# FFN transform over 512 blocks of 4 tokens, Toeplitz products in four row groups of the array

## The chip, the core and the metric

The kernel runs on one core of one Trainium2 chip. The metric is device time in microseconds (us) for one launch, the median of several runs. The launch contains two layers; the change touches only the second part of the second layer and the steps that prepare it.

## What is computed

The first layer is a windowed attention block on a (2, 128, 64, 64) image. The second layer is a self-attention over the same 4096 tokens of each of two images, followed by a spectral FFN. The change concerns the FFN. Cut to what matters:

```
# u: (2, 4096, 128); phi: (4096, 16); K = 16 filters
U_plus [b,t,k,d]  = sum_s phi[t-s, k] * u[b,s,d]             # causal convolution in time
U_minus[b,t,k,d]  = (-1)^t * sum_s phi[t-s, k] * (-1)^s u[b,s,d]
out[b,t,e] = sum_k sum_d U_plus*sigma_k^0.25*Mpp[k,d,e] + U_minus*sigma_k^0.25*Mpm[k,d,e]
out += three short lags of u times Mu[lag];   one of 4 branch weights per segment of tokens
```

Even and odd times are kept apart (the parity `par`, 2048 tokens each), so that plus and minus share one set of products.

## The kernel before

**How the convolution is tiled.** Each parity's 2048 tokens are CB = 256 blocks of FB = 8 tokens. Along the blocks a Fourier transform of length NC = 320 is taken (a matmul with a table `tr`), which leaves BINS = 160 complex bins. For each bin the convolution inside a block is a small Toeplitz product; then the 16 filters are contracted with the mixed matrices `mpl` and `mmi`, and the bins go back to tokens with a matmul against `inv`.

**Where the pieces run.**

- `after(b, c, part)` (16 calls, spread through the attention of layer 2 as filler work, one yielded piece at a time) normalises 512 tokens, transposes them, does the forward transform and stores the bins to the DRAM tensor `us`. Each call makes two 512-wide products per half table (L1034), copies them out by DVE and ACT (L1036) and stores them, with a smaller remainder (L1044, L1050).
- `filters()` transforms the filter taps (L1195), sums them (L1202, L1205) and stores them to the DRAM tensor `gs`.
- `short_lags` adds the three short lags into the residual `xa` (L1082, L1089).
- `group()` loads nothing itself: `blocks(q)` and `inputs(q)` have loaded `ct` (Toeplitz blocks) and `ut` (transformed tokens) four pairs of bins ahead. For each of 2 pairs of bins, 2 parities and 2 images it makes two 64-row Toeplitz products of 512 columns, one in each half of the array's rows (L1381), each into its own PSUM tile `pc`. DVE copies one, ACT the other, into `y` (L1382). The `ps_c` pool has 6 PSUM tiles.
- `project` contracts one of the 16 filters for a group of GB = 4 bins: 256 columns at full array (L1393), 16 with `mpl` and 16 with `mmi` into one PSUM tile `acc`; the last one is followed by one ACT copy into `ob` (L1400).
- `back_into` (32 calls in two steps each, slipped between projections from group 16 on) takes 64 bins back into the residual: 2 transposes (L1409), an ACT copy, 2 products of 256 columns (L1415), one DVE addition (L1417).
- The tail turns the last 32 bins (L1456), adds them and the residual (L1466, L1470, L1474, L1475) and stores the output in four DMAs of 1 MB.

**Other lines that are referred to.** L509 is the score product of the first layer's windowed attention (32 rows, four heads), L604 a 128-column product there; L383 and L398 are small DVE operations of a layer norm there. In the second layer, L905 is the attention's score product, L929 turns a tile of its exponentials by TensorE, L932 copies that out and sums it by DVE, and L943 and L970 are the products with the tokens. In `after`, L1002 is a DVE operation of 128 elements and L1015 the ACT copy of the transposed tokens into `zc`, with 32 bytes between words.

**What sets the order.** TensorE's order in the FFN is written out by hand (`manual_schedule`): first the Toeplitz products of group g+1, then the 32 projections of group g, and so on for 40 groups. DVE's and ACT's instructions stand in the order of the program text. All loads and stores of this part are issued on SP's queue.

Of the kernel before, what the change touches and what calls it, by code (L numbers as in the profile page):

```python
# [82 lines left out]
CB, FB, SG = 256, 8, 4  # L83
SB = CB // SG
NC = CB + SB

CHUNKS = (0, 1, 4, 5, 2, 3, 6, 7)
BINS = NC // 2
GB = 4
BC = 64  # L90
LG = 2 * FB
GROW = 4 * LG * KF


@with_exitstack
def kernel(
# [100 lines left out]
    def token_tiles(b, n0, pt):  # L197
        for j in range(4):
            ph, f = divmod(n0 + j, FB)
            par, h = divmod(ph, 2)  # L200
            t0 = h * TH + 2 * f + par
            nc.tensor.transpose(
                pt[:, j * P : (j + 1) * P], xa[b][:, t0 : t0 + 2 * FB * (P - 1) + 1 : 2 * FB], ident
            )
# [21 lines left out]
    with l0a:  # L226
# [449 lines left out]
        halves = [n0 for h in range(2) for n0 in range(0, NT, 4) if n0 // FB % 2 == h]  # L676
# [177 lines left out]
    t_in, t_filter, t_out = _transforms()  # L854


    us = dram.tile([BINS, 2, SG, FB, NB, 2, P], F32, name="us")
    gs = dram.tile([BINS, 2, SG, GROW], F32, name="gs")

    with ap_:  # L860
# [10 lines left out]

        tr = tp.tile([P, 2, NC], F32, name="tr")
        nc.sync.dma_start(out=tr, in_=nc.inline_tensor(t_in, "t_in").ap().rearrange("(h p) c -> p h c", p=P))
# [116 lines left out]
        def after(b, c, part):  # L990

            n0 = 4 * c
            ph, f0 = divmod(n0, FB)
            par, h = divmod(ph, 2)
# [6 lines left out]
            for j in range(4):  # L1001
# [12 lines left out]
            s0 = 1 + h * (TH // 2)  # L1014
            nc.scalar.copy(  # L1015
                zc[b][:, par, s0 : s0 + TH // 2].rearrange("p (c f) -> p f c", f=FB)[:, f0 : f0 + 4, :],
                pt.rearrange("p (f c) -> p f c", f=4),
            )
            yield
            z2 = z.rearrange("p f d -> p (f d)")  # L1020

            def store(m0, q, src):
                nc.sync.dma_start(
                    out=us[m0 // 2 : (m0 + P) // 2, :, 2 * h + q, f0 : f0 + 4, b, par, :].rearrange(
                        "g r f d -> (g r) f d"
                    ),
                    in_=src.rearrange("p (f d) -> p f d", d=P),
                )

            for m0 in (0, P):  # L1030
                for q in range(2):
                    rows_ = slice(q * SB, (q + 1) * SB)
                    pu = bank()
                    nc.tensor.matmul(pu, lhsT=tr[rows_, h, m0 : m0 + P], rhs=z2[rows_], start=True, stop=True)  # L1034
                    ub = sp.tile([P, 512], F32, tag="ub", name="ub", bufs=3)
                    (nc.scalar.copy if q else nc.vector.tensor_copy)(ub, pu)  # L1036
                    store(m0, q, ub)
                yield

            banks = [bank() for q in range(2)]  # L1040
            for i in range(2):
                for q in range(2):
                    rows_ = slice(q * SB, (q + 1) * SB)
                    nc.tensor.matmul(  # L1044
                        banks[q][i * 64 : (i + 1) * 64, 0:256], lhsT=tr[rows_, h, 2 * P : NC],
                        rhs=z2[rows_, i * 256 : (i + 1) * 256], start=True, stop=True,
                    )
            ub = sp.tile([P, 512], F32, tag="ub", name="ub", bufs=3)
            for q in range(2):
                (nc.scalar.copy if q else nc.vector.tensor_copy)(ub[:, q * 256 : (q + 1) * 256], banks[q][:, 0:256])  # L1050
                for i in range(2):
                    nc.sync.dma_start(
                        out=us[P:, :, 2 * h + q, f0 + 2 * i : f0 + 2 * i + 2, b, par, :].rearrange("g r f d -> (g r) f d"),
                        in_=ub[i * 64 : (i + 1) * 64, q * 256 : (q + 1) * 256].rearrange("p (f d) -> p f d", d=P),
                    )
# [7 lines left out]
        def short_lags(b, h):  # L1063


            for par in range(2):
                n0 = (par * 2 + h) * FB
                for f0 in range(0, FB, 4):
                    pt = bank()
                    transposed(pt, tt[b][:, n0 + f0 : n0 + f0 + 4, :])  # L1070
                    nc.scalar.copy(xa[b][:, (n0 + f0) * P : (n0 + f0 + 4) * P], pt)
                    yield
            for par in range(2):
                n0 = (par * 2 + h) * FB
                xv = xa[b][:, n0 * P : (n0 + FB) * P].rearrange("p (f c) -> p f c", f=FB)
                for c0 in range(0, P, 64):
                    py = lag_bank()
                    for lag in range(3):
                        from_par = (par - lag) % 2
                        back = (lag - par + from_par) // 2  # L1080
                        s0 = 1 + (h * P + c0) * FB - back
# [3 lines left out]
                    pv = py.rearrange("p (c f) -> p f c", f=FB)  # L1085
                    first = h == 0 and c0 == 0
                    for lo, hi, s in ((0, 32, 0), (32, 64, 1)) if first else ((0, 64, 2 + h),):
                        xs = xv[:, :, c0 + lo : c0 + hi]
                        nc.vector.scalar_tensor_tensor(  # L1089
                            xs, pv[:, :, lo:hi], seg[:, s : s + 1], xs, ALU.mult, ALU.add  # L1090
                        )
# [75 lines left out]
        def filters():  # L1167
# [44 lines left out]
            for slot in range(begin[-1] + SG):  # L1212
                mine = [(m, slot - s0) for m, s0 in enumerate(begin) if 0 <= slot - s0 < SG]
                for mj in mine:
                    more(*mj)
# [359 lines left out]
```

## Time and profile before

| what | us |
|---|---|
| median of 3 runs | 2191.98 (2191.19 to 2192.96) |
| span of the profiled execution, first to last instruction | 2190.3 |
| TensorE busy | 2142.9 (98%) |
| DVE busy / ACT busy / GpSimd busy | 953.2 / 769.8 / 278.7 |
| before the FFN's first Toeplitz product | 0 to about 1284 |
| FFN, 40 groups | about 1284 to 2165 |
| tail | about 2165 to 2190 |

The profile holds one execution; the median of the runs is 1.7 us above its span. In the profile a 32-bit float matmul shows as two records, each preceded by a weight load (PEld), so that counts of matmuls there are twice those of the program text. A group's line gives the number of instructions, the busy time, the mean duration of one in ns, and the idle time of its engine just before them with what ended that idle time.

### The profile page before, as it was taken

Reading aid. Unit: us, or ns where it says so; the run is one execution under the profiler, and the core shown is the slowest. Engines: PE = TensorE matmul, PEld = TensorE weight load, DVE = VectorE, ACT = ScalarE, POOL = GpSimd, SP = SyncE. Lnnn points to the kernel's source line nnn. Section 1 sums busy time; section 2 is a strip of 40 time slices with the busy share of each in tenths; the row PEclk is TensorE's granted clock in tenths of the full one; section 3 lists DMA queues with packets and bytes.
Section 4 is the critical chain, followed back from the end, with each engine's and each line's share of the span. In section 5 each row is a group of like instructions: output and inputs, shape, how many; then the busy total and the mean of one; then the engine's idle time right before and its main releaser. Section 6 shows DMA issues by size and latency. Waiting matters only on the chain.

```text
span 2190.3 us, 32068 instructions
## 1 busy us (share of the span) xinstructions
PE 2142.9 (98%) x12016; PEld 1341.7 (61%) x12016; DVE 953.2 (44%) x3150; ACT 769.8 (35%) x1904; POOL 278.7 (13%) x359
## 2 busy tenths in 40 slices
PE   6899999999999999999999999999999999999998
PEld 4677765545555544544555456776767676767776
DVE  5899986444443353366333543222232323232232
ACT  3889883222332232122223223223232323232232
POOL 3477874200000000000000000000000000000000
PEclk8999999999999999999999999999999999999999
DMA  4222212011000010042000132121221212222101
GB/s 147 61 62 62 61 53 53 0 68 53 25 24 25 24 49 25 0 139 87 0 24 26 47 112 56 44 60 45 55 56 44 53 47 48 53 46 54 40 10 77
DMA packets 170347, 110.56 MB, mean 50 GB/s; under 512 B 21311, under 2 KB 155087, under 8 KB 169680
## 3 DMA queue, kind: packets, MB, share of 16 engines
q1 hardware_dynamic: 169266, 105.01, 17.7%
q8 instruction: 95, 1.56, 0.3%
q0 software_dynamic: 576, 2.10, 0.3%
q10 hardware_dynamic: 350, 1.41, 0.2%
q14 instruction: 60, 0.49, 0.1%
HBM read 73.86 MB, written 34.63 MB: 50 GB/s over the span
## 4 chain that ended last, share of the span: by engine, by line
PE 87%; DVE 5%; POOL 3%; DMA 2%; ACT 1%; issue 1%; SPq 0%; ACTq 0%; POOLq 0%; DVEq 0%
PE acc L1393 26%; PE pc L1381 13%; PE own L943 10%; PE bank L905 9%; PE other L970 8%; PE bank L929 4%; PE bank L335 2%; PE bank L1082 2%; PE bank L545 2%; PE bank L195 2%; PE bank L1034 1%; PE py L1415 1%; DMA st<-in_m_minus_dram 1%; PE bank L509 1%; PE po L567 1%; ACT p L532 1%
## 5 line engine op out<-in xcount | busy, mean ns | idle before, releaser
L1382 DVE COPY y<-pc 128x512 f32<-128x512 f32 x320 | 221.5, 692 | 350.7 <-PE pc L1381 347.0
L913 ACT ACTIVATE e<-bank 128x512 f32<-128x512 f32 (+3 forms) x288 | 161.6, 561 | 510.0 <-PE bank L905 393.6
L1393 PE MATMUL acc<-y,mpl 128*128 128x256 f32 x1280 | 292.2, 383 | 0.0
L1393 PE MATMUL acc<-y,mmi 128*128 128x256 f32 x1280 | 288.1, 380 | 0.0
L1381 PE MATMUL pc<-ct,ut 64*128 64x512 f32 x1280 | 285.5, 596 | 0.0
L905 PE MATMUL bank<-cm 128*128 128x512 f32 (+3 forms) x576 | 277.5, 564 | 1.4 <-DVE y L656 1.4
L1393 PEld LDWEIGHTS acc<-y,mpl 128*128 128x128 f32 x1280 | 238.8, 190 | 58.7 <-issue 29.5
L1393 PEld LDWEIGHTS acc<-y,mmi 128*128 128x128 f32 x1280 | 243.3, 191 | 31.9
L1382 ACT COPY y<-pc 128x512 f32<-128x512 f32 x320 | 204.6, 640 | 92.3 <-PE pc L1381 92.2
L943 PE MATMUL own<-et,tok 128*128 128x512 f32 x448 | 227.8, 595 | 4.2 <-DVE part L932 4.2
L970 PE MATMUL other<-e,tok 128*128 128x512 f32 x448 | 229.1, 593 | 0.3 <-DVE xa L982 0.3
L1381 PEld LDWEIGHTS pc<-ct,ut 64*128 64x128 f32 x1280 | 120.7, 187 | 145.8 <-issue 140.6
L932 DVE CUSTOM_DVE_ANT_0 et<-bank,one 128x512 f32<-128x512 f32 x224 | 146.0, 687 | 120.3 <-PE bank L929 120.2
L1400 ACT COPY ob<-acc 128x256 f32<-128x256 f32 x32 | 19.0, 594 | 387.0 <-PE acc L1393 387.0
L943 PEld LDWEIGHTS own<-et,tok 128*128 128x128 f32 x448 | 84.0, 190 | 113.5 <-issue 66.6
L1417 DVE TENSOR_TENSOR xa<-py,xa 128x512 f32<-128x512 f32 x32 | 22.2, 693 | 281.4 <-PE py L1415 281.4
L970 PEld LDWEIGHTS other<-e,tok 128*128 128x128 f32 x448 | 82.0, 191 | 89.9 <-issue 87.1
L929 PEld LDWEIGHTS bank<-ident,e 128*128 128x128 f32 x896 | 102.8, 141 | 54.3 <-issue 49.0
L905 PEld LDWEIGHTS bank<-cm 128*128 128x128 f32 x576 | 94.1, 191 | 64.5 <-issue 44.1
L167 POOL TENSOR_TENSOR ln_rs<-ln_rs,mhalf 128x4 f32<-128x4 f32 x24 | 24.2, 1007 | 773.4 <-DVE ln_rs L166 773.4
L532 ACT ACTIVATE p<-p,mn 128x196 f32<-128x196 f32 x256 | 114.4, 449 | 13.6 <-DVE mn L522 13.1
L929 PE MATMUL bank<-ident,e 128*128 128x128 f32 x896 | 117.3, 274 | 0.0
(227 smaller groups left out, 2344.3 us busy)
## 6 DMA issues: line engine op xcount, KB each, us to landing
ut<-us SPq DMA_DIRECT2D x80, 256.0 KB
us<-ub SPq DMA_DIRECT2D x64, 256.0 KB
vw<-vd SPq DMA_DIRECT2D x256, 49.0 KB
ct<-gs SPq DMA_DIRECT2D x160, 72.0 KB
ct<-gs SPq DMA_DIRECT2D x160, 64.0 KB
gs<-sum SPq DMA_DIRECT2D x20, 256.0 KB
vd<-v SPq DMA_DIRECT2D x128, 32.0 KB
st<-in_m_plus_dram SPq DMA_DIRECT2D x16, 256.0 KB
```

Of the source, the lines that this page charges most:

```text
L195: nc.tensor.transpose(ps[:, j * P : (j + 1) * P], src[:, j, :], ident)
L335: nc.tensor.matmul(pl, lhsT=wg[:, lo : lo + P], rhs=zT, start=True, stop=True)
L532: nc.scalar.activation(p, p, AF.Exp, bias=t[name + "mn"][:, h : h + 1], scale=-1.0, accum_out=t["den"][:, u, h : h + 1],)
L905: nc.tensor.matmul(ps[:, lo:], lhsT=cm[b][:, n * P : (n + 1) * P], rhs=cm[b][:, CHUNKS[c] * 512 + lo : (CHUNKS[c] + 1) * 512], start=True, ...
L913: nc.scalar.activation(e[:, lo:], ps[:, lo:], AF.Exp, bias=0.0, scale=ASCALE, accum_out=part[:, n, c : c + 1])
L929: nc.tensor.transpose(pt[:, k * P : (k + 1) * P], es[k][:, m * P : (m + 1) * P], ident)
L932: nc.vector.tensor_tensor_reduce(et, pt, one, 1.0, 0.0, ALU.mult, ALU.add, part[:, n, a : a + 1])
L943: nc.tensor.matmul(own, lhsT=tok[b][:, n, :], rhs=e, start=first, stop=last)
L970: nc.tensor.matmul(other, lhsT=tok[b][:, 4 * CHUNKS[a] + j, :], rhs=es[j], start=(j == 0), stop=(j == 3))
L1381: nc.tensor.matmul(pc, lhsT=ut[fp, b, par, :], rhs=cv_[fp], start=True, stop=True)
L1382: (nc.scalar.copy if f else nc.vector.tensor_copy)(y[:, 4 * f : 4 * f + 4, :, par, b * 2 * FB + q : (b + 1) * 2 * FB : 2], pc.rearrange("p ...
L1393: nc.tensor.matmul(acc, lhsT=(mmi if l else mpl)[:, k, :], rhs=y[:, 1::2, k, ::-1, :] if l else y[:, 0::2, k, :, :], start=(l == 0 and k = ...
```

## The change

The sizes change: FB = 4 tokens to a block, CB = 512 blocks, NC = 640, K2 = 80 steps over quadruples of bins (a group is still two loads, 40 groups).

- **Forward transform, radix 2.** Even and odd blocks are transformed apart (`tr` has a table for each, e = 0, 1) and combined as sum and difference. In `after`, each bank of PSUM holds both halves; ACT copies one half to SBUF (`half`), DVE makes the sum and the difference (`ub`), and there are 16 stores per call on SP's queue where there were 8. In `filters`, the sums are made by ACT and DVE as before, the sum and difference and a negated copy by GpSimd, with 32 stores where there were 20.
- **Toeplitz products in four row groups.** `burst` makes, per load and parity, 2 images x 4 bins of 32-row products of 256 columns; the four bins j go to four row groups and four PSUM tiles `pcs[j]`. Each tile is full after both images and is then copied into `y` by DVE (j even) or ACT (j odd). Per group there are two bursts, one ahead of the 16 `mpl` projections and one ahead of the 16 `mmi` projections.
- **`y` changes its layout**: the bin is now the innermost index, with 8 of them, so a copy writes words 32 bytes apart (they were 8 bytes apart).
- **Backward transform, radix 4.** `mixed_bins` replaces the copy after a group's last projection: one ACT copy of 256 columns, then eight DVE operations (two of 128 elements, two of 64, four of 32) that write the four quarters into `ob`.
- `back_into` has 16 calls, with 4 transposes, one ACT copy of 512, 4 products of 128 columns and 2 DVE additions of 256. The tail turns 16 remaining quadruples and adds them in 32-row products of 64 columns.

```diff
-CB, FB, SG = 256, 8, 4
+FB, SG = 4, 4
+CB = TH // FB
...
-GB = 4
+KG = 8 // FB
+GB = 4 * KG
...
         def after(b, c, part):
...
-            for m0 in (0, P):
-                for q in range(2):
-                    rows_ = slice(q * SB, (q + 1) * SB)
-                    pu = bank()
-                    nc.tensor.matmul(pu, lhsT=tr[rows_, h, m0 : m0 + P], rhs=z2[rows_], start=True, stop=True)
-                    ub = sp.tile([P, 512], F32, tag="ub", name="ub", bufs=3)
-                    (nc.scalar.copy if q else nc.vector.tensor_copy)(ub, pu)
-                    store(m0, q, ub)
-                yield
+            def store(pu, n, r0, m, ri):
+                for s in range(2):
+                    half = sp.tile([P, 256], F32, tag="uo", name="uo", bufs=2)
+                    nc.scalar.copy(half[:, 0:n], pu[s][:, n : 2 * n])
+                    ub = sp.tile([P, 2, 256], F32, tag="ub", name="ub", bufs=4)
+                    for sgn, op in enumerate((ALU.add, ALU.subtract)):
+                        nc.vector.tensor_tensor(ub[:, sgn, 0:n], pu[s][:, 0:n], half[:, 0:n], op)
+                    for sgn in range(2):
+                        to = us[r0 : r0 + m, sgn, :, 2 * hh + s, 2 * fp : 2 * fp + 2, b, par, :]
...
-        def group(other=None):
-            y = cp.tile([P, 8, KF, 2, 32], F32, tag="y", name="y", bufs=2)
-            for q in range(GB // 2):
+        def burst(y, i):
+            for kl in range(i * (KG // 2), (i + 1) * (KG // 2)):
                 ct, ut = ahead.pop(0)
...
+                for pars in at_once:
+                    pcs = [ps_c.tile([P, 4, 2 * len(pars), TK], F32, tag="pc", name="pc") for _ in range(4)]
+                    for x, (par, b) in enumerate((par, b) for par in pars for b in range(NB)):
+                        cv_ = ct[:, :, 0 : 2 * (FB + 1 + par) * KF].rearrange("p o (l c) -> p o l c", l=2)[:, :, :, 0:TK]
+                        for j in range(4):
+                            rows_ = slice(32 * j, 32 * j + 32)
+                            nc.tensor.matmul(
+                                pcs[j][:, :, x, :], lhsT=ut[rows_, b, par, :], rhs=cv_[rows_], start=True, stop=True
                             )
+                    for j in range(4):
+                        if FB == 4:
+                            to = y[:, :, :, pars[0], :, 4 * kl + j]
...
+                        (nc.scalar.copy if j % 2 else nc.vector.tensor_copy)(
+                            to, pcs[j].rearrange("p l x (t k) -> p l k (x t)", k=KF)
+                        )
...
+        def new_y():
+            return cp.tile([P, 4, KF, 2, 2 * FB, GB], F32, tag="y", name="y", bufs=2)
...
+        def mixed_bins(g, acc):
+            af = cp.tile([P, 256], F32, tag="af", name="af", bufs=2)
+            nc.scalar.copy(af, acc)
+            av = af.rearrange("p (m s) -> p m s", s=2)
+            sd = cp.tile([P, 2, 128], F32, tag="sd", name="sd", bufs=2)
+            for s, op in enumerate((ALU.add, ALU.subtract)):
+                nc.vector.tensor_tensor(sd[:, s, :], av[:, :, 0], av[:, :, 1], op)
...
+            nc.vector.tensor_tensor(to[0], sv[:, 0], sv[:, 1], ALU.add)
+            nc.vector.tensor_tensor(to[1], sv[:, 0], sv[:, 1], ALU.subtract)
+            nc.vector.tensor_tensor(to[2][:, 0], dv[:, 0, 0], dv[:, 1, 1], ALU.subtract)
+            nc.vector.tensor_tensor(to[2][:, 1], dv[:, 0, 1], dv[:, 1, 0], ALU.add)
+            nc.vector.tensor_tensor(to[3][:, 0], dv[:, 0, 0], dv[:, 1, 1], ALU.add)
+            nc.vector.tensor_tensor(to[3][:, 1], dv[:, 0, 1], dv[:, 1, 0], ALU.subtract)
...
-            for g in range(BINS // GB):
-                following = group() if g + 1 < BINS // GB else None
-                acc = ps_p.tile([P, 64 * GB], F32, tag="acc", name="acc")
+            for g in range(GROUPS):
+                following = new_y() if g + 1 < GROUPS else None
+                acc = ps_p.tile([P, 256], F32, tag="acc", name="acc")
                 for l in range(2):
+                    if following is not None:
+                        burst(following, l)
                     for k in range(KF):
                         project(g, y, acc, l, k)
-                        if rest and k in ((3, 11) if g >= 2 * BC // GB else (7,)):
+                        if rest and k in (5, 13):
                             if next(rest[0], None) is None:
                                 rest.pop(0)
+                mixed_bins(g, acc)
                 y = following
```

The rest of the diff carries the new sizes through the token order (`token_tiles`, `short_lags`), the filter stores, the tables and the tail. In the compiled order of the changed kernel, DVE's eight operations of `mixed_bins(g)` stand ahead of the copies of the burst that follows group g's last projection.

## The prediction

> **What bounds the kernel now.** I read the page's busy line and chain first, then the chain of waits inside a stretch of the FFN, then the timeline at the start of one group.
>
> ```profile
> PE 2142.9 (98%) x12016; PEld 1341.7 (61%) x12016; DVE 953.2 (44%) x3150; ACT 769.8 (35%) x1904; POOL 278.7 (13%) x359
> ```
>
> ```profile
> 8 pieces in order of time: start us, us, what
> ...
> 1469.46 14.01 PE acc L1393 x64
> 1483.47 7.07 PE pc L1381 x32
> 1490.54 14.01 PE acc L1393 x64
> 1504.55 7.07 PE pc L1381 x32
> ```
>
> TensorE is never idle in the FFN: a group is 7.07 us of Toeplitz products and 14.01 us of projections, 21.08 us, 40 times. In the groups (line, engine, tile, shape; busy us, mean ns; idle before), DVE and ACT wait for TensorE, never the reverse:
>
> ```profile
> L1381 PE MATMUL pc<-ct,ut 64*128 64x512 f32 x1280 | 285.5, 596 | 0.0
> L1382 DVE COPY y<-pc 128x512 f32<-128x512 f32 x320 | 221.5, 692 | 350.7 <-PE pc L1381 347.0
> L1382 ACT COPY y<-pc 128x512 f32<-128x512 f32 x320 | 204.6, 640 | 92.3 <-PE pc L1381 92.2
> L509 PE MATMUL bank<-kT,qT 32*64 32x196 f32 x1024 | 43.3, 359 | 1.1 <-DVE mn L522 0.8 <-ACT pT L552 0.2
> ```
>
> The timeline shows what a group begins with; the copies start about 1.2 us after the products (1505.68 against 1504.48), here 0.03 to 0.07 us after the record of the product they need ends:
>
> ```profile
> 1504.48 3.28 PE L1381 MATMUL pc<-ct,ut 64*128 64x512 f32 x14
> 1504.59 0.59 ACT L1400 COPY ob<-acc 128x256 f32<-128x256 f32 x1 [13.34 <-PE acc L1393]
> ...
> 1505.68 0.64 ACT L1382 COPY y<-pc 128x512 f32<-128x512 f32 x1 [0.50 <-PE pc L1381]
> 1505.71 1.48 DVE L1382 COPY y<-pc 128x512 f32<-128x512 f32 x2 [14.45 <-PE pc L1381]
> ```
>
> **What the skill says.** "TensorEngine Tiling (Array Packing)", Performance Considerations: after a 4x speedup of TensorE the PSUM copy may become the bottleneck. In this trace two row groups already halve the time and the copies (692 and 640 ns) fit inside a pair's 2 x 442 ns; with four row groups they no longer do. "TensorE: Matmul & The Clock Gate", Part 3, gives 3.07x for four 32-row products. The trace has 32-row products too: L509 takes 43.3 us for 512 products of 196 columns, 85 ns each; at full array they would take 196 / 256 x 432 = 331 ns (64 records of L1393 come every 0.216 us), so the trace shows 3.9x. I use four. "Vector Engine (DVE) Microarchitecture Reference", 5.2, says a stream whose every element lands away from the last is slower: 1.71 ns per column for a destination hopping 4 KiB, 2.50 for steps of 24 words, against 1.05. The trace agrees in kind: L1015 writes words 32 bytes apart, L1475 16 bytes apart, and both cost about 400 ns more than 512 contiguous words (L1417, 693):
>
> ```profile
> L1417 DVE TENSOR_TENSOR xa<-py,xa 128x512 f32<-128x512 f32 x32 | 22.2, 693 | 281.4 <-PE py L1415 281.4
> L1475 DVE TENSOR_TENSOR o<-py,xa 128x512 f32<-128x512 f32 x8 | 8.8, 1102 | 12.9 <-PE py L1470 11.3 <-DMA out_dram<-o 1.6
> L1015 ACT COPY zc<-bank 128x512 f32<-128x512 f32 x8 | 8.7, 1082 | 17.2 <-PE bank L195 17.2
> ```
>
> **Part 1: Toeplitz products and their copies.** The new `y` is written 32 bytes apart. So an ACT copy costs 1.08 us (L1015, the same step) and a DVE copy 1.10 us (L1475). Bounds: 0.69 us if the step costs nothing; 512 x 2.50 + 160 = 1.44 us at the page's worst rate, 160 ns being what 693 leaves over 512 x 1.04.
>
> A burst has 2 parities of 8 products in 4 tiles. One image's four products are two waves of records, each 256 columns, 0.216 us (L1393), so a parity is four waves; the first wave of a switch shows 0.32. The last wave starts at 0.32 + 0.216 x 2 = 0.75 and its record lasts 0.38: tiles are full at 1.13 us. There are 6 PSUM tiles. The second parity takes the two free ones at once, but its third product waits for DVE's copy of the first tile, and behind it on TensorE stand the rest of the burst and 16 projections. Undisturbed, DVE starts at 1.16, ends at 2.26, TensorE resumes at 2.32 (0.06 for the signal, as between the ends and starts above) and needs 0.32 + 3 x 0.216 = 0.97: burst 3.29 us.
>
> For the burst after a group's last projection DVE is not free. `mixed_bins` stands ahead in its queue: ACT starts 0.11 after the switch (L1400), 0.37 for 256 contiguous columns (L1050), DVE begins at 0.52. Two operations of 128 elements at 0.26 (pitch of L1002's), two of 64 at about 0.19, four of 32 at about 0.13 (between L398's 0.17 and L383's pitch of 0.07) and 0.15 for two waits on its own results give 1.57: DVE is free at 2.1, its copy ends at 3.2, TensorE resumes at 3.26, burst 4.2 us.
>
> Both bursts: 7.5 us against 7.07, although the products alone would take 3.5. Projections are unchanged at 14.0. That is +0.43 x 39 groups = **+17 us**. With the copy at 0.69 us the bursts are 2.88 and 3.8, -0.4 x 39 = -16; at 1.44 us they are 3.63 and 4.55, +1.1 x 39 = +43. Loads (`ct`, `ut`): as many on SP's queue, `ct` half the bytes, issued four loads ahead; hidden behind the projections.
>
> **Part 2: back into the residual.** Before, 32 places of 2 transposes (0.109 each) and 4 records of 0.216: 1.08 x 32 = 35 us on TensorE, on the path. After, 16 places of 4 transposes and 8 records of 0.112 (the pitch of L604's 128-column records): 1.33 x 16 = 21. **-13 us**. The ACT copy and DVE additions lie beside projections.
>
> **Part 3: before the FFN.** Columns in `after` are the same on TensorE. DVE's work grows from 2 x 0.69 + 0.43 = 1.8 us to 8 x 0.36 + 4 x 0.22 = 3.8 a call, 16 calls, +32 us, and `short_lags` splits each addition in four, +0.4 x 16. In 700 to 1284 us DVE is below half busy and TensorE idles little, so attention's products cover it, except where a queued attention operation of DVE comes late. `filters` saves about 5 us of columns (20 x 512 to 24 x 256, two at a time) but makes DVE wait up to 1.8 us for GpSimd's sums six times; behind DVE stand attention's turned tiles (L932), for which L943 waits. I set these against each other with +3. The last `after` calls have no cover: SP issues 16 stores at 0.4 to 0.6 us (before, 8), so the first `ut` load, behind them on SP's queue, goes some 3 us later. Sum **+6 us**, bounds -4 and +22 (a fifth of DVE's added work exposed, and the end twice as long).
>
> **Part 4: tail.** The last `mixed_bins` takes 2.1 us where an ACT copy took 0.6 before the transposes (L1456): +1.5. Four output steps of 4 banks each, out of 6, wait for the previous step's copies (3 x 0.6 us of strided words): about +0.5 each, and the last copies end 1 us later. **+4 us**, bounds 0 and +8.
>
> **Sum.** +17 - 13 + 6 + 4 = +14 us on a span of 2190.3; with the 1.7 by which the median stands above it, **2206 us**. A measurement of this kernel can tell about 0.2%, 4.4 us, from no change.
>
> **Rivals.**
> - *The copies keep their speed* (0.69 us, ACT alike). For it: the step of 8 bytes in the old `y` costs DVE nothing. Against: L1015 and L1475. Then -16 - 13 + 6 + 4 = -19: 2173 us. This decides the sign: with everything else as above, the break-even is a DVE copy of about 0.92 us (each 0.1 us is 0.1 x 78 = 8 us). Chance, with a shorter `mixed_bins` or full cover in part 3, 0.2.
> - *Copies at the worst rate*, +43 instead of +17: 2232 us. For it the page's 2.50; against it that all strided rows here stand near 1.1. Chance 0.15, with DVE's added work exposed in the attention (+15).
> - *The four row groups do not run together*, only two at a time: each parity 0.86 us longer, partly under the copy's wait, +0.9 x 78 = +70: about 2275 us. L509's rows speak against it. 0.05.
> - *No visible change*, the gains of part 2 meeting the losses: 2187.6 to 2196.4, 0.1.
>
> **How the numbers follow.** The likeliest case, 2196 to 2225, has 0.5; slower in all 0.7, same 0.1, faster 0.2. Its own range is 2196 to 2225; 8 in 10 need the lower half of the worst-rate case and the nearer half of the faster one: 2177 to 2245.
>
> **What would show it.** Right: L1424 products with 4 starts within some 20 ns, TensorE idle before or within L1424 released by DVE's L1432, about 0.9 us in one burst and 1.8 in the other; L1432 near 1.1 us on both engines; L1483 half of L1415's time; a group of about 21.5 us. Wrong: L1432 near 0.7 us, or bursts near 3 us, or new idle time of L943 before 1284 us beyond some 10 us.

## The result, and the profile after

The changed kernel takes 2207.6 us (median of 4 runs, 2206.5 to 2211.0); the kernel before takes 2192.5 beside it. The ratio is 1.0070, 95% interval 1.0055 to 1.0084: 0.7% slower. The profiled execution has a span of 2206.3 us, 16.0 more than before's 2190.3. The prediction was 2206.

The page of the changed kernel, its busy line and its costliest groups (busy us, mean ns of one; idle us before them and what ended it):

```profile
PE 2068.9 (94%) x13704; PEld 1376.1 (62%) x13704; DVE 1111.1 (50%) x3680; ACT 872.6 (40%) x1942; POOL 306.9 (14%) x391
...
L1432 ACT COPY y<-pc 128x512 f32<-128x512 f32 x320 | 317.8, 1109 | 308.8 <-PE pc L1424 295.0
L1432 DVE COPY y<-pc 128x512 f32<-128x512 f32 x320 | 313.3, 1081 | 222.6 <-PE pc L1424 222.6
...
L1424 PE MATMUL pc<-ct,ut 32*128 32x256 f32 x2560 | 220.6, 404 | 78.1 <-DVE y L1432 74.9
```

TensorE was busy for 98% of the span and is now busy for 94%. Its Toeplitz products cost less, but it stands idle among them for 78.1 us, and 74.9 of these end when DVE has copied a full tile into `y`. The copies went from 692 and 640 ns to 1081 and 1109.

The chain of waits of the changed kernel over one group of the FFN (start us, us, what):

```profile
1480.88 0.38 ACT af L1452
...
1481.29 0.49 DVE sd L1456 x2
...
1482.46 0.99 DVE y L1432
...
1483.50 1.13 PE pc L1424 x12
1484.63 7.10 PE acc L1444 x32
1491.73 1.11 PE pc L1424 x16
1492.85 1.06 DVE y L1432
...
1493.95 1.17 PE pc L1424 x12
1495.12 1.06 PE acc L1444 x4
```

Before, this chain was TensorE alone. Now each of the two bursts passes through DVE: the second through one copy of 1.06 us, the first through ACT's copy of `acc`, `mixed_bins` and then the copy. Between them stand 7.10 us for 16 projections (32 records of the profile).

The difference of 16.0 us, placed by three moments that both traces show:

| moment | before, us | after, us | stretch up to it, after less before | predicted |
|---|---|---|---|---|
| first Toeplitz product | 1283.9 | 1295.6 | +11.7 | +6 |
| last projection | 2164.0 | 2179.6 | +3.9 (FFN 880.1, now 884.0) | +17 - 13 = +4 |
| end of the span | 2190.3 | 2206.3 | +0.4 | +4 |

The first row compares one execution with one. In e1_rows, e2_spread and e3_later, whose program is the changed kernel's up to there, the first Toeplitz product lies at 1294.3, 1296.4 and 1291.9 us, so the +11.7 can be anything from +8 to +12.5.

### The profile page after: what moved, and what is told of

Read it like the earlier page. It is cut to its first block, busy times and chain, and to the rows that moved or that the text cites. A ratio compares the mean times of both kernels' runs of the same rounds, so it can differ in the third digit from the quotient of the medians.

```text
span 2206.3 us, 36375 instructions
## 1 busy us (share of the span) xinstructions
PE 2068.9 (94%) x13704; PEld 1376.1 (62%) x13704; DVE 1111.1 (50%) x3680; ACT 872.6 (40%) x1942; POOL 306.9 (14%) x391
## 3 DMA queue, kind: packets, MB, share of 16 engines
q1 hardware_dynamic: 180738, 94.13, 15.2%
## 4 chain that ended last, share of the span: by engine, by line
PE 70%; DVE 12%; issue 9%; DMA 4%; POOL 3%; ACT 2%; SPq 1%; POOLq 0%; DVEq 0%; ACTq 0%
PE acc L1444 18%; PE own L958 10%; PE bank L920 9%; PE other L985 7%; PE pc L1424 6%; DVE y L1432 4%; PE bank L944 4%; PE bank L345 2%; PE bank L555 2%; PE bank L203 1%; PE bank L1060 1%; DMA st<-in_m_plus_dram 1%; DMA st<-in_m_minus_dram 1%; PE bank L519 1%; PE bank L1103 1%
## 5 line engine op out<-in xcount | busy, mean ns | idle before, releaser
L1432 ACT COPY y<-pc 128x512 f32<-128x512 f32 x320 | 317.8, 1109 | 308.8 <-PE pc L1424 295.0
L1432 DVE COPY y<-pc 128x512 f32<-128x512 f32 x320 | 313.3, 1081 | 222.6 <-PE pc L1424 222.6
L1424 PE MATMUL pc<-ct,ut 32*128 32x256 f32 x2560 | 220.6, 404 | 78.1 <-DVE y L1432 74.9
L1444 PEld LDWEIGHTS acc<-y,mmi 128*128 128x128 f32 x1280 | 238.7, 190 | 43.2 <-issue 12.9
L1424 PEld LDWEIGHTS pc<-ct,ut 32*128 32x128 f32 x2560 | 149.2, 185 | 145.0 <-DVE y L1432 108.0
L542 ACT ACTIVATE p<-p,mn 128x196 f32<-128x196 f32 x256 | 114.4, 449 | 12.9 <-DVE mn L532 12.3
L1456 DVE TENSOR_TENSOR sd<-af 128x128 f32<-128x128 f32 x80 | 19.7, 288 | 194.6 <-ACT af L1452 194.6
L1452 ACT COPY af<-acc 128x256 f32<-128x256 f32 x40 | 14.9, 372 | 212.9 <-issue 164.9
```

Of the source, the lines that this page charges most:

```text
L542: nc.scalar.activation(p, p, AF.Exp, bias=t[name + "mn"][:, h : h + 1], scale=-1.0, accum_out=t["den"][:, u, h : h + 1],)
L1424: nc.tensor.matmul(pcs[j][:, :, x, :], lhsT=ut[rows_, b, par, :], rhs=cv_[rows_], start=True, stop=True)
L1432: (nc.scalar.copy if j % 2 else nc.vector.tensor_copy)(to, pcs[j].rearrange("p l x (t k) -> p l k (x t)", k=KF))
L1444: nc.tensor.matmul(acc, lhsT=(mmi if l else mpl)[:, k, :], rhs=y[:, l::2, k, ::-1] if l else y[:, l::2, k], start=(l == 0 and k == 0), sto ...
```

## The experiments

My theory after the result had two halves. In the FFN, the copies' 32-byte steps and DVE's queue ahead of them hold TensorE. Ahead of the FFN, where the miss lies, I suspected first DVE's added work, then SP's added stores, then the buffers of the matrix loads. Line numbers of experiments can differ by one or two from those of the changed kernel.

### Is it the 32-byte step? (e1_rows)

```diff
-                            to = y[:, :, :, pars[0], :, 4 * kl + j]
+                            to = y[:, :, :, pars[0], 4 * kl + j, :]
...
-            return cp.tile([P, 4, KF, 2, 2 * FB, GB], F32, tag="y", name="y", bufs=2)
+            return cp.tile([P, 4, KF, 2, GB, 2 * FB], F32, tag="y", name="y", bufs=2)
```

ACT's copy of `acc` restores the order.

> Only the layout of y is changed: bin ahead of block position, so that a copy writes runs of 8 adjacent words; the ACT copy of acc puts the columns back in the old order. Theory (the 32-byte step doubles the copies, and the copies hold the PSUM tiles for which the second parity waits): L1432 falls to about 0.69 us on DVE and 0.64 on ACT, each burst shortens by about 0.4 us (3.39 and 3.83 to about 3.0 and 3.4), 78 bursts, -31 us: about 2176 us, faster than the kernel before the change (2192). Rival (the copies are slow because DVE and ACT write the same tile at once, or read PSUM with a 64-byte step): L1432 stays at 1.1 us, time within 5 us of 2207.

Measured: 2174.0 us, ratio to before 0.9912 (0.9896 to 0.9929). The page of e1_rows, the groups of the copies:

```profile
L1432 DVE COPY y<-pc 128x512 f32<-128x512 f32 x320 | 205.8, 684 | 262.7 <-PE pc L1424 262.6
L1432 ACT COPY y<-pc 128x512 f32<-128x512 f32 x320 | 171.9, 589 | 377.3 <-PE pc L1424 377.3
```

The copies are at their old speed with the same number of elements, the bursts fall from 3.83 and 3.39 us to 3.44 and 2.97, and TensorE's idle time in the products behind DVE's copies from 74.9 to 44.9. DVE and ACT still write one tile at once and still read PSUM with the same step, so the rival of the expectation falls. The step of 32 bytes costs some 400 ns a copy on DVE and 520 on ACT, and it decides the sign of the whole change: without it the kernel is 0.9% faster than before, with it 0.7% slower.

### Does TensorE need to wait for a copy at all? (e2_spread)

The two parities of a burst, which stood one behind the other, stand eight projections apart.

```diff
-                    if following is not None:
-                        burst(following, l)
                     for k in range(KF):
+                        if following is not None and k % 8 == 0:
+                            burst(following, l, (k // 8,))
                         project(g, y, acc, l, k)
```

> Only TensorE's order is changed: the two parities of a burst are put 8 projections apart, instead of one behind the other; copies and layout as they were. Theory (the gain of four row groups goes into a wait for PSUM tiles): TensorE's idle time in L1424 (78 us) is gone, four half bursts of 0.97 to 1.05 us and four runs of 8 projections of 3.55 us give a group of about 18.3 us instead of 21.4, -3.1 x 39 = -121 us: about 2086 us. Rival (the loss is in the switches between 32-row and 128-row products): twice as many switches at about 0.2 us each add 0.4 x 39 = 16 us: about 2223 us. Rival (DVE and ACT become the bound): 10.3 us of DVE copies and sums a group would have to grow to 18, which is not expected.

Measured: 2110.5 us, ratio to before 0.9620 (0.9606 to 0.9634). The chain of waits of e2_spread in the FFN:

```profile
1470.26 1.08 PE pc L1424 x16
1471.34 3.65 PE acc L1446 x16
1474.99 1.07 PE pc L1424 x16
1476.06 3.65 PE acc L1446 x16
```

The chain is TensorE alone again, although the copies still take 1086 and 1115 ns: a tile now has 3.65 us to be emptied. The FFN takes 785.3 us, 98.7 less than in the changed kernel, against some 121 expected, which allowed too little for changing between 128-row and 32-row products: the 16 records of a half burst (8 products of 256 columns in four row groups) are four waves of 0.216 us, 0.86, and take 1.08; the 16 records of 8 projections are 3.46 and take 3.65. A round trip thus costs 0.41 us, and a group now makes four where it made two. More PSUM tiles would be another way to keep TensorE from waiting; no run tried it.

### Both remedies (e6_rows_spread)

> Both remedies together: the bin stands ahead of the block position in y, so that a copy writes 32 B runs (684 ns on DVE and 589 on ACT where the changed kernel needs 1081 and 1109), and the two halves of a burst stand eight projections apart. Theory (with the halves apart the copies lie wholly beside TensorE's work, whose own time is then the bound): no further gain, median within 3 us of the 2110.5 of the halves apart alone. Rival (the two gains add, since copies still hold TensorE or its row groups somewhere): some 30 us less, near 2080.

Measured: 2107.7 us, ratio to before 0.9606 (0.9589 to 0.9623), FFN 784.4 against 785.3. The copies are back at 686 and 590 ns and nothing is gained in the FFN. A copy's duration matters only while TensorE waits for it.

### The longer burst: mixed_bins ahead of the copies (e3_later, e7_pool_bins)

e3_later moved `mixed_bins` in the program text behind the next burst:

```diff
+                    if l == 0 and g:
+                        mixed_bins(*waiting)
...
-                mixed_bins(g, acc)
+                waiting = (g, acc)
```

> Only the place of mixed_bins is changed: its ACT copy and eight DVE operations stand behind the copies of the burst that follows, instead of ahead. Theory (DVE's sums delay the first copy, for which TensorE waits): every second burst falls from 3.83 to 3.39 us, -0.44 x 39 = -17 us: about 2190 us. Rival (the longer burst comes from something else, such as the wait for the last projection): no change, 2207 us.

Measured: 2205.1 us, ratio to before 1.0055 (1.0040 to 1.0070), FFN 884.0 as in the changed kernel. The timeline of e3_later on DVE shows why this decides nothing:

```profile
1477.57 0.49 DVE L1456 TENSOR_TENSOR sd<-af 128x128 f32<-128x128 f32 x2 [5.94 <-ACT af L1452]
...
1478.56 0.18 DVE L1468 TENSOR_TENSOR ob<-sd 128x32 f32<-128x32 f32 x1
1478.66 3.89 DVE L1432 COPY y<-pc 128x512 f32<-128x512 f32 x4
```

DVE's operations stand ahead of the copies as before, although the text now has them behind. So it does not hold here that DVE's and ACT's instructions stand in the order of the program text, as was said ahead of the prediction. The next kernel takes them off DVE instead:

```diff
+            eng = nc.gpsimd if g + 1 < GROUPS else nc.vector
...
-            nc.vector.tensor_tensor(to[0], sv[:, 0], sv[:, 1], ALU.add)
+            eng.tensor_tensor(to[0], sv[:, 0], sv[:, 1], ALU.add)
```

(and likewise for the other seven).

> The eight sums and differences of mixed_bins are issued on GpSimd for all groups but the last, so that DVE has nothing ahead of a burst's copies. Theory (the burst after a group's last projection is longer than the other one only because mixed_bins keeps DVE until 1.65 us after the burst's start): both bursts take 3.4 us, 39 x 0.44 = 17 us less in the FFN (884.0 -> 867), median near 2190. Rival (the two bursts differ by something else, such as ACT's copy of acc, or GpSimd's operations slow DVE's copies): bursts stay at 3.8 and 3.4, or both rise; median 2205 or more.

Measured: 2192.5 us, ratio to before 0.9997 (0.9990 to 1.0004). The bursts take 3.44 and 3.39 us, the FFN 868.8, 15.2 less than in the changed kernel. The timeline of e7_pool_bins at the burst that was the longer one:

```profile
1474.89 1.56 PE L1424 MATMUL pc<-ct,ut 32*128 32x256 f32 x20
...
1475.53 0.76 POOL L1457 TENSOR_TENSOR sd<-af 128x128 f32<-128x128 f32 x2 [18.88 <-ACT af L1452]
1476.11 3.92 DVE L1432 COPY y<-pc 128x512 f32<-128x512 f32 x4 [6.60 <-ACT af L1452]
...
1477.24 1.16 PE L1424 MATMUL pc<-ct,ut 32*128 32x256 f32 x12 [0.78 <-DVE y L1432]
```

and the same of the changed kernel:

```profile
1480.73 1.56 PE L1424 MATMUL pc<-ct,ut 32*128 32x256 f32 x20
...
1482.38 3.89 DVE L1432 COPY y<-pc 128x512 f32<-128x512 f32 x4
1483.50 1.13 PE L1424 MATMUL pc<-ct,ut 32*128 32x256 f32 x12 [1.20 <-DVE y L1432]
```

DVE's copy starts 1.22 us after the burst (in the changed kernel 1.65) and TensorE resumes after 2.35 (2.77). GpSimd beside it does not slow DVE's copies: 1084 ns. So what made one burst longer than the other was `mixed_bins` on DVE, and its 0.4 us per group are 15 of the FFN's microseconds.

### Ahead of the FFN: is it DVE's added work? (e5_plain_after)

Each half's sums and differences in `after` give way to one plain copy, so the FFN's input is not the transform's; ACT's extra copy goes too.

```diff
-                    for sgn, op in enumerate((ALU.add, ALU.subtract)):
-                        nc.vector.tensor_tensor(ub[:, sgn, 0:n], pu[s][:, 0:n], half[:, 0:n], op)
+                    (nc.scalar.copy if s else nc.vector.tensor_copy)(
+                        ub[:, :, 0:n], pu[s][:, 0 : 2 * n].rearrange("p (e n) -> p e n", e=2)
+                    )
```

> Leaves out the sums and differences of the forward transform of the tokens: each PSUM tile in after is copied out whole, one by DVE and the next by ACT, as in the kernel before; stores, products and their order stay. Theory (DVE's added work in after makes attention's DVE operations late): of the 11.7 us by which the first Toeplitz product comes later than before, the 5 to 6 us that appear during the second image's attention go away: the product starts near 1289 us instead of 1295.6. Rival (the filter matrices' loads or SP's stores delay it): no change, 1295 us.

Measured, one run: 2205.3 us, first Toeplitz product at 1294.1 us against 1295.6. Where this part of the program is unaltered (e1_rows, e2_spread, e3_later and the changed kernel), the same product lies anywhere from 1291.9 to 1296.4, so 1.5 us is no effect that this can tell. TensorE's idle time is the sharper measure: over the four stretches of the table further below it is 27.9 us, as in e1_rows (28.0) and e2_spread (27.9). So the sums that `after` adds to DVE are covered by the attention's products. The additions of `short_lags`, which are split as well, stayed as they were.

### Ahead of the FFN: is it SP's added stores? (e4_one_store, e8_spread_one)

One DMA carries the sums and the differences of a half.

```diff
-                    for sgn in range(2):
-                        to = us[r0 : r0 + m, sgn, :, 2 * hh + s, 2 * fp : 2 * fp + 2, b, par, :]
+                    to = us[r0 : r0 + m, :, :, 2 * hh + s, 2 * fp : 2 * fp + 2, b, par, :]
...
-                            nc.sync.dma_start(
-                                out=to[:, ri], in_=ub[:, sgn, :].rearrange("p (f d) -> p f d", d=P)
-                            )
+                        nc.sync.dma_start(
+                            out=to[:, :, ri], in_=ub.rearrange("p g (f d) -> p g f d", d=P)
+                        )
```

> The sums and the differences of a half, which the changed kernel stores with two DMAs from SP's queue, leave in one DMA of twice the size; nothing else changes. Theory (SP's queue is what makes the FFN start 11.7 us later than before, since its 8 + 8 last issues take 8.5 us and the loads of the mixing matrices and of the first ut stand behind such issues): with half the issues the first Toeplitz product comes 4 to 8 us before the changed kernel's 1295.6 us, the wait for ut before it (3.25 us) falls below 1, and the median is near 2201. Rival (SP's time goes by the rows that an issue describes, or the delay lies in the order of the attention's work and not in SP): first Toeplitz product within 2 us of 1295.6, median within 3 us of 2207.6.

> The halves of a burst eight projections apart and one DMA for the sums and differences of a half. Theory (the late start of the FFN comes from SP's issues): 4 to 8 us less than the 2110.5 of the halves apart alone, near 2104. Rival (it does not): 2108 to 2113.

Measured: e4_one_store 2208.9 us, ratio to before 1.0070 (1.0052 to 1.0087), first Toeplitz product at 1300.0; e8_spread_one 2109.0 us, 0.9615 (0.9600 to 0.9630), against 2110.5 of the spread alone. The timeline of SP's queue at the end of the last `after` call, the changed kernel first, then e4_one_store:

```profile
1279.96 4.11 SPq L1045 DMA_DIRECT2D us<-ub  x8
1284.16 4.44 SPq L1050 DMA_DIRECT2D us<-ub  x8
1292.76 2.24 SPq L1405 DMA_DIRECT2D ut<-us  x5
```

```profile
1285.02 2.75 SPq L1044 DMA_DIRECT2D us<-ub  x4
1288.15 4.32 SPq L1049 DMA_DIRECT2D us<-ub  x4
1297.31 2.24 SPq L1404 DMA_DIRECT2D ut<-us  x5
```

and the kernel before:

```profile
1270.84 3.60 SPq L1023 DMA_DIRECT2D us<-ub  x4
1274.74 2.55 SPq L1052 DMA_DIRECT2D us<-ub  x4
1279.28 2.24 SPq L1360 DMA_DIRECT2D ut<-us  x5
```

With half as many issues, the way from the first of these stores to the load of `ut` is 12.3 us in place of 12.8, although SP's own time for them falls only from 8.6 to 7.1. The kernel before, with stores of the same number and size as e4_one_store (four of 256 KB, four of 64 KB), needs 8.4. So the number of issues does not set it. In both later kernels SP is done over 4 us ahead of the load, which waits until the stores have landed. What they land at is in the DMA view of the changed kernel from 1279 to 1296 us (40 equal slices; busy share of the 16 DMA engines in tenths, and what they moved):

```profile
DMA  1000677987779821111111111111110000639998
GB/s 42 22 13 0 190 219 228 286 269 217 218 234 293 254 66 30 43 43 42 43 43 43 42 37 39 43 33 27 43 31 22 5 0 0 48 106 352 381 357 318
```

The stores of full row tiles (L1045) run at 190 to 290 GB/s; those of the leftover rows (L1050) at about 43, with a tenth of the engines busy, from 1285 to 1292 us. These 8 stores of 32 KB, not their issue, hold the first load. From the first store of leftover rows to the load it takes 8.6 us, in the kernel before 4.5 for as many bytes. Their form differs: the outermost index of such a store has 2 values in the changed kernel and 64 in the kernel before. No run changed that form alone, so this last step is read from the traces and not tested.

That the product comes at 1300.0 us in e4_one_store, later than in any trace with separate stores, has its place in the attention: from 950 to 1040 us TensorE idles 10.8 us there and 10.3 in e8_spread_one, where traces with separate stores and two buffers have 6.1 to 7.8. Why larger stores cost that is open.

### Ahead of the FFN: buffers of the matrix loads (e9_deep, e10_before_deep, e11_spread_deep)

The loads of the mixing matrices (`st`) get six buffers of their own in place of two, in the changed kernel, in the kernel before and beside the spread.

```diff
+            with tc.tile_pool(name="mixing", bufs=6) as mix:
+                yield from filter_matrices(mpl, mmi, mix)
             ctp = ctx.enter_context(tc.tile_pool(name="blocks", bufs=5))
...
-            yield from filter_matrices(mpl, mmi)
```

> The changed kernel, where filter_matrices' loads (st) have six buffers of a pool of their own in place of two, and the pool of the first ct blocks is opened behind it. Theory (in the second image's attention VectorE, in order, stands at the mixing of a loaded matrix, whose load could only start when one of two buffers came free, and the attention's copies and sums behind it are late for TensorE): VectorE's waits for st shrink from some 23 us to below 8, TensorE's idle time from 950 to 1040 us falls from 7.8 to below 4, the first Toeplitz product comes near 1291 in place of 1295.6, median near 2203. Rival (the delay there has another cause, such as the order in which the work is placed): idle time there stays above 6, first Toeplitz product within 2 us of 1295.6.

> The same six buffers in the kernel before the change, whose TensorE idles 3.9 us from 950 to 1040 us. Theory (the buffers hold both kernels, the changed one by some 4 us more): idle time there falls to some 2, first Toeplitz product from 1283.9 to near 1282, median within 3 us of 2192.5, so that the two kernels lie closer than before. Rival (the buffers are worth the same in both): the same gain here as in the changed kernel.

> The two halves of a burst eight projections apart, and the six buffers. Theory: the gain before the FFN adds to that of the spread: 2110.5 less 4 to 5, near 2106. Rival: 2109 to 2112.

Measured: e9_deep 2201.9 us, ratio to before 1.0033 (1.0025 to 1.0040), first Toeplitz product at 1291.3; e10_before_deep 2189.1 us, 0.9977 (0.9969 to 0.9984), at 1279.6; e11_spread_deep 2104.6 us, 0.9588 (0.9569 to 0.9606), at 1290.7. The waits of DVE from 940 to 1060 us (in total, times, longest), first of the changed kernel:

```profile
DVE mpl L1178 <- DMA st<-in_m_plus_dram: 12.1, 6, 4.5
DVE mmi L1178 <- DMA st<-in_m_minus_dram: 8.4, 10, 1.6
```

and of e9_deep:

```profile
DVE mpl L1178 <- DMA st<-in_m_plus_dram: 5.7, 1, 5.7
...
DVE mpl L1176 <- DMA st<-in_m_plus_dram: 1.1, 1, 1.1
```

The loads no longer follow each release of a buffer, and TensorE's idle time from 950 to 1040 us falls from 7.8 to 3.9. As a mechanism this holds. As the cause of the difference between the two kernels it explains little: between e9_deep and e10_before_deep the first Toeplitz product still lies 11.7 us apart. By that moment both kernels gain 4.2 us, as the rival in the expectation of e10_before_deep had it; but this is one trace of each, and the moment scatters by as much. By idle time in the stretch the changed kernel gains 3.9 and the kernel before 2.1, so at most some 2 us of the difference lie in these buffers.

### All of it, and the filter sums (e12_all)

Beside the three remedies, each sum in `filters` goes to the other of two buffers:

```diff
-                sums = sp.tile([P, 2, LL], F32, tag="fsum", name="fsum", bufs=1)
                 for j in range(SG):
...
+                    last = whole if j else None
+                    sums = sp.tile([P, 2, LL], F32, tag="fsum", name="fsum", bufs=2)
```

What led to it is on the timeline of the changed kernel, DVE from 499 to 504 us:

```profile
498.92 0.68 DVE L1245 TENSOR_TENSOR fsum<-bank,fsum 64x512 f32<-64x512 f32 x1 [1.77 <-POOL fb L1248]
501.96 0.68 DVE L1245 TENSOR_TENSOR fsum<-bank,fsum 64x512 f32<-64x512 f32 x1 [2.37 <-POOL fb L1248]
502.57 0.67 DVE L997 TENSOR_TENSOR xa<-other,xa 128x512 f32<-128x512 f32 x1
```

DVE stands at the filter's addition until GpSimd has read the previous sum, and the attention's addition (L997) behind it is what TensorE waits for.

> The remedies together: halves of a burst eight projections apart, the bin ahead of the block position in y, six buffers for filter_matrices' loads, and in filters() each sum of a row tile written to the other of two buffers (uo gives up one of its two for the space), so that VectorE's next addition does not stand behind GpSimd's reading of the last. Theory (TensorE's wait of 2.5 us at 503 us, with VectorE's sum of another product standing behind such an addition, comes from that single buffer): TensorE's idle time from 440 to 950 us falls from 5.9 to some 3.5, the first Toeplitz product comes 2 us before the 1290.7 of the spread with six buffers, median near 2100. Rival (GpSimd's 2.9 us for each sum are the pace, whatever the buffers): the wait stays, median 2102 to 2105.

Measured: 2099.7 us, ratio to before 0.9578 (0.9562 to 0.9594), the lowest median, though its interval overlaps that of e11_spread_deep. First Toeplitz product at 1285.8, 4.9 us before that of e11_spread_deep. TensorE's waits from 440 to 950 us, first of the changed kernel, then of e12_all:

```profile
PE other L985 <- DVE xa L997: 2.5, 1, 2.5
PE own L958 <- DVE part L947: 1.7, 3, 0.7
```

```profile
PE own L958 <- DVE part L947: 2.8, 3, 1.3
PE bank L934 <- ACT e L928: 0.8, 1, 0.8
```

The wait of 2.5 us is gone and two of 1.2 and 1.3 behind `part` have grown, so the idle time of this stretch falls by 1.4 (5.99 in e11_spread_deep, 4.56), not by the 2.4 expected. The 4.9 us are therefore not all that one wait's. The traced execution is also the fastest of the four, and it alone of the changed kernels' traces has the full granted clock of TensorE at the start of the FFN (see below).

## Why the prediction was right, and where it was not

**The mechanism and the sign** were as the likeliest case had them: copies at the strided rate, TensorE idle behind them twice a group. What the Trainium skill's "TensorEngine Tiling (Array Packing)", Performance Considerations, says of the PSUM copy, that it may become the bottleneck, describes this kernel: 74.9 us of TensorE's idle time end with such a copy.

**The sum** is closer than its terms: +16 us for +14, with the groups 4 us below what was said, the FFN's start 4 above, the stretch before the FFN 6 above and the tail 4 below.

**Part 1, size of the copies.** Predicted 1.10 (DVE) and 1.08 us (ACT), measured 1.081 and 1.109. Rows of other lines that write with a step gave nearly the right price, although DVE's row had a step of 16 bytes and not of 32. The prediction's "about 400 ns more" for ACT set ACT's row against a contiguous one of DVE; against ACT's own contiguous copy the step costs 520. The rival "copies keep their speed" stood at 2173 us; e1_rows, which gives them back their speed, measured 2174. The worst rate (1.44 us) is excluded by the measured copy.

**Part 1, the bursts.** The undisturbed burst: TensorE resumes after 2.29 us (2.32 predicted) and needs 1.10 more (0.97), in all 3.39 for 3.29. The burst behind `mixed_bins`: predicted 4.2, measured 3.83, and the mis-sized term is `mixed_bins` itself. DVE begins 0.56 us after the switch (0.52 predicted), but the eight operations take 1.09 and not 1.57, since the next one of 128, 64 or 32 elements starts after about 0.2, 0.14 and 0.10 us; DVE is free at 1.65 and not at 2.1. Left out of the sum was that the projections are entered twice from 32-row products: 2 x 7.10 for 14.01, +0.19. The group is 3.83 + 3.39 + 14.20 = 21.42 us against 21.08: +0.34 x 39 = +13, where +17 stood.

**Part 2.** L1483 takes half of what L1415 took, as said:

```profile
L1483 PE MATMUL py<-inv,t 128*128 128x128 f32 x128 | 16.9, 275 | 0.0
```

(a row of the groups of the changed kernel; before, 32.9 us.) Counted from the start of each product to the start of the next, the transposes and products of `back_into` hold TensorE for 34.6 us before and 21.2 after: -13.4, where -13 stood.

**The FFN as a whole** grew by 3.9. With +13 for the groups and -13 for part 2, some +4 is left, and it lies at the FFN's start, for which the prediction had no term. In the 20 us from the first Toeplitz product the granted clock of TensorE was 1.00 before and is 0.75 now (each line gives the stretch, its length, the busy time and records of TensorE, its weight loads, DVE, ACT and GpSimd, then the granted clock, the DMA share and GB/s):

```profile
1283.86:1303.86 20.00, 20.00 (x85) 9.86 (x85) 12.58 (x18) 10.23 (x16) 0.00 (x0) 1.00 0.41 104
```

```profile
1295.56:1315.56 20.00, 18.96 (x113) 11.72 (x114) 12.86 (x16) 11.81 (x12) 0.00 (x0) 0.75 0.28 84
```

The six records of `short_lags` that stand there, the same products in both kernels, take 2.84 us before and 5.19 now:

```profile
1285.78 2.84 PE L1082 MATMUL py<-tt,mu 128*128 128x512 f32 x6
```

```profile
1300.92 5.19 PE L1103 MATMUL py<-tt,mu 128*128 128x512 f32 x6
```

e6_rows_spread and e12_all have the same program in the FFN, and a granted clock of 0.83 and 1.00 over these 20 us; their FFNs take 784.4 and 781.4 us. So the groups cost 4 us less than predicted, the start 4 us that the prediction had at nothing, and the FFN's +4 came out exact by luck.

**Part 3** is the step that failed in size: +11.7 for +6 (with the scatter of that moment, +8 to +12.5), inside its bounds of -4 to +22. TensorE's idle time from 300 us to the first Toeplitz product, in four stretches:

| stretch, us | before | after | after, six buffers | before, six buffers |
|---|---|---|---|---|
| 300 to 440 | 7.5 | 9.5 | 9.7 | 8.1 |
| 440 to 950 | 1.9 | 5.9 | 5.9 | 1.9 |
| 950 to 1040 | 3.9 | 7.8 | 3.9 | 1.8 |
| 1230 to the first Toeplitz product | 3.2 | 5.8 | 5.3 | 3.2 |

(From 1040 to 1230 us it has none in any of the four.) The sum, before rounding, grows from 16.4 to 29.1. The prediction had +3 for the attention and +3 for the end. The end is +2.6 (last row), of the right size for a wrong reason: it put it on SP's 16 issues, and e4_one_store shows that their number doesn't set it. The attention has the miss, some +10 of idle time in place of +3, of which some 2 are made up elsewhere (the last product with `cm` comes 8.1 us later than before: 1252.4 for 1244.3). Of its named suspects, DVE's added sums in `after` are cleared (e5_plain_after), the split additions of `short_lags` were not tried; the wait for GpSimd's sums was named and priced against the saving in `filters`, and it is there (2.5 us at 503 us). For 950 to 1040 the buffers of the matrix loads hold both kernels (six of them take 7.8 to 3.9 and 3.9 to 1.8), and why the changed one suffers more, as well as where the 2 us before 440 come from, stays open: DVE takes up its work in a different order in the two traces, and no run isolated that.

**Part 4**: +0.4 for +4. What the last `mixed_bins` and the output steps add is nearly all made up for within the tail; no run took it apart.

**The rival of two row groups at a time** falls with four starts within 20 ns (1470.242 to 1470.262 us for the first wave) and later waves every 0.216 us, which is also the distance between two full-array records of 256 columns. So waves in a row make four products in the time of one. The Trainium skill's 3.07x for four 32-row products of 512 columns ("TensorE: Matmul & The Clock Gate", Part 3) is lower than that and near what a short run gives here: in e2_spread 16 records take 1.08 us where 16 at full array would take 3.46, 3.2x with the switches.

**"What would show it."** L1432 near 1.1 us, L1483, the starts and the group came as listed. The waits of 0.9 and 1.8 us show as 0.73 and 1.20 between the records of the page's products, since a product's record runs on while the next could start.

## What to carry to other kernels

When a product becomes four times faster, put its copies on the timeline first: what counts is whether a tile is full and empty again before TensorE needs it, and work of another kind placed between two halves of a burst (here eight projections) buys that time for the price of a switch; it brought 97 us where faster copies brought 34. A layout that makes a copy write with a step should be priced by a row of the same step in the same trace, on both engines. Small operations that end a phase belong on an idle engine if the next phase's copies stand behind them, and moving them in the program text alone may move nothing.

## What the runs showed that I had not expected

- The FFN's start can meet a lower granted clock. In the traces of the changed kernel and of all its variants but e12_all, TensorE waits 2.76 to 3.95 us for the first load of `ut`, and within 2.5 us of the end of that wait the granted clock falls to half for 6.8 or 10.2 us. In e12_all, where it waits 2.45 us, and in the two traces of the kernel before, where it does not wait, the clock stays full there. Behind the earlier wait of 2.5 us near 503 us stands a stretch of 3.4 us at half clock in nine of eleven traces, and behind one of 2.9 us (e9_deep, ending at 961 us) none, so the length of the wait alone does not decide it; no run took it apart.
- A change between 128-row and 32-row products costs about 0.2 us each way (0.41 for the round trip: 1.08 for 0.86 and 3.65 for 3.46). In e2_spread, with four round trips a group, that is 1.6 of the group's 18.9 us.
- ACT gains more than DVE from contiguous writes: 1109 to 589 ns, against 1081 to 684, for the same 512 columns.
- Eight small DVE operations take 1.09 us although their durations add up to 1.74: each starts before the record of the last one ends.
- Merging two stores of 128 KB into one of 256 KB shortens SP's issue (4.11 to 2.75 us), but the eight stores of 32 KB from leftover rows move 43 GB/s with a tenth of the DMA engines busy, and four of 64 KB of the same form (e4_one_store) are no sooner done.
